# Seeds that stay in PSUM over several gathers, and relu sums divided between ScalarE and VectorE, in a two-layer graph kernel

## The chip, the cores and the metric

The kernel runs on one core of one Trainium2 chip. The metric is the device time in microseconds; the figure of a kernel is the median of its runs. Of the kernel before there are three: 1049.07, 1049.10 and 1049.19 us.

## What is computed

Two graph layers, each followed by a residual sum and a layer norm over 64 features, for 128 graphs ("batches") of 128 nodes. Only the first layer matters here:

```
mask = (adj > 0)
diff = x[:, :, None, :] - x[:, None, :, :]
h    = relu((x @ W1a)[:, :, None, :] + diff @ W1b + b1)      # 192 wide
hm   = einsum('bjkh,bjk->bjh', h, mask)
x    = layernorm(x + hm @ W2 + deg[..., None] * b2)
```

With u = x @ (W1a + W1b) + b1 and v = -(x @ W1b), h is relu(u_j + v_k), summed over the neighbours k of node j. The second layer is a small message-passing step with a gated update; the change does not touch what it computes.

## The kernel before

**Tiling.** Nodes lie on the 128 partitions. Batches go in 32 groups of four (G = 4). The 128 possible neighbours of a node are cut into two halves of 64, and in each half the neighbours are ranked. The first eight of a half (W0) have fixed slots; those beyond go to overflow segments of four slots (W1), 128 segments a batch.

**Values and pieces.** `values` (L539) makes u and v, and 2 x 64 further columns that carry v @ W2/2 and u @ W2/2, in a PSUM tile `pu` of 512 columns, and copies it to `uv`. `pieces` (L556) splits v (with its 64 further columns) into three bf16 tiles b0, b1, b2 whose sum is v: two casts on ScalarE (L563, L569) and two subtractions on GpSimd (L566, L572).

**Picks.** `picks` (L529) makes one-hot bf16 matrices by comparing ranks: `pick0` for the eight fixed slots (from `rankT`), `pick1` for the four overflow slots (from `place`), one VectorE instruction of 512 columns per slot and group. `past` and `own` (L480, L481) say which overflow segment belongs to which node; `own32` is a GpSimd cast of `own` (L487), `ownT` its transpose, `us` the u of each segment's owner (`over`, L602).

**The core: seed, gather, reduce.** For each batch there are six stretches of two slots (C = 2): four of fixed slots, two of overflow slots. For each stretch ScalarE copies u four times (two halves, two slots) into a PSUM tile `pv` of two banks (`seeds`, L597); TensorE adds the neighbours' v by 12 matmuls, pick by piece (`gathers`, L628); VectorE sums the absolute values over the four into a part of 192 columns (`reduces`, L644). There are three `pv` tiles in a ring (`ps_g`, bufs=3), so a seed waits until the reduce three stretches before has read its tile. Relu comes from relu(z) = (z + |z|)/2: the sum of |z| is this path's; the sum of z is linear, and enters in `second` by three matmuls per batch of the mask with the further columns of b0 to b2 (`sums_of_z`, L705, L708), and by a GpSimd product of deg with uv's last columns (`others`, L492). Empty slots hold u alone; `base` (L656) makes their number times |u|, which `together` subtracts.

**Joining.** `together` (L663) is four GpSimd instructions per batch (384, then 192, 192 and 192 columns). `sums` (L677) transposes the part by a matmul and adds the overflow part by `ownT`, and `second` (L296) multiplies by W2, adds the residual and starts the layer norm, half of it on GpSimd. The rest of the tail (`turn`, `message1` to `message3`, `gates`, `update`) is layer two.

**The order** is written out by hand. Each part is a generator; TIMETABLE gives a due time for each of its steps, in units of which PER = 768 make a group, and FIRST and SETUP give those of the beginning. All steps of all groups are sorted by due time and issued in that order, each engine then executing its own instructions in it. Steps of up to seven groups are interleaved. SP issues all loads and stores.

Of the kernel before, what the change touches and what calls it, by code (L numbers as in the profile page):

```python
# [8 lines left out]
F32 = mybir.dt.float32  # L9
# [7 lines left out]
F = 64  # L17
# [4 lines left out]
V = H + F  # L22
W0 = 8
W1 = 4
C = 2
BIGR = 2.0 ** 23
# [3 lines left out]
PER = 768  # L30
TIMETABLE = {
    "load": (-1520,), "masks": (-559,), "ranks": (-122, -122), "degrees": (-402, -367), "turned": (-19, -1),
    "counts": (-114,), "offsets": (-22, -22, 80, 228, 245, 348, 349), "owners": (1039, 1066), "places": (368, 431),
    "pieces": (337, 538, 550, 595), "others": (1085, 1194), "values0": (-55, -50, -37), "values1": (204, 204, 268),
    "pick0": (-44, 50, 88, 133, 133, 137, 251, 419), "pick1": (663, 679, 679, 679), "over0": (578, 602),
    "over2": (1053, 1123), "base0": (693,), "together0": (728, 840, 1185, 1275), "sums0": (1392, 1392, 1405),
    "base1": (708,), "together1": (1189, 1219, 1289, 1289), "base2": (443,), "together2": (1345, 1353, 1370, 1370),
    "sums2": (1443, 1449, 1449), "base3": (717,), "together3": (1408, 1417, 1417, 1417),
    "second": (1425, 1453, 1473, 1502, 1502, 1503), "turn": (1504, 1504), "message1": (1512, 1512),
    "message2": (1534, 1538), "message3": (1539, 1696), "gates": (2002, 2032, 2052, 2068, 2068, 2080),  # L40
    "update": (2201, 2201, 2333, 2396, 2584, 2918, 3390, 3734, 4832),
    "seed": (644, 644, 657, 674, 684, 685, 711, 728, 728, 741, 761, 837, 923, 937, 978, 1149, 1149, 1173, 1203, 1221,
        1271, 1326, 1395, 1397),
    "gather": (661, 661, 681, 681, 686, 708, 730, 730, 737, 748, 767, 940, 1026, 1051, 1110, 1161, 1163, 1189, 1238,
        1317, 1338, 1405, 1405, 1405),
    "reduce": (664, 678, 684, 684, 706, 724, 740, 743, 780, 862, 894, 947, 1119, 1138, 1138, 1192, 1215, 1233, 1263,
        1358, 1358, 1407, 1407, 1407),
# [3 lines left out]
SETUP = (-8001, -7999, -7610, -7530, -7400, -7380, -700, -690)  # L51
FIRST = {
    "load": (-8000, -7998), "masks": (-7580,), "ranks": (-7520, -7515), "degrees": (-7389, -7388), "counts": (-7387,),
    "offsets": (-7372, -7371, -7366, -7366, -7366, -7366, -7365), "turned": (-7359, -7358),
    "values0": (-7375, -7374, -7370), "values1": (-7368, -7364, -7360), "pieces": (-7373, -7363, -7355, -7350),
    "places": (-7357, -7356), "pick0": (-7512, -7512, -7512, -7512, -7365, -7365, -7365, -7365),
    "pick1": (-7352, -7352, -7351, -7351), "over0": (-7349, -7348), "seed": (-7369, -7366, -7361, -7354),
    "gather": (-7367, -7362, -7354, -7351), "reduce": (-7365, -7358, -7353, -7350),
}

# [3 lines left out]
def adj_resnorm_kernel(  # L80
# [42 lines left out]
    wall = const.tile([N, 4 * N], F32, name="wall")  # L123
# [3 lines left out]
    wT = const.tile([HC, 4, 2, F], F32, name="wT")  # L127


    NBI = V + 256 + F  # L130
# [3 lines left out]
    call3, bias3, gb2 = three[:, 0:V], three[:, V : V + 256], three[:, V + 256 : NBI]  # L134
# [27 lines left out]
    def setup(ps_g, ps_w):  # L162
# [8 lines left out]
        for h in range(2):  # L171
            spread(bias[h * F : h * F + 3, 0:H], b1)
            spread(bias[h * F : h * F + 3, H:V], b2)
# [28 lines left out]
        nc.vector.tensor_scalar_mul(wall[:, V : V + H], wab[:, 1, :], -1.0)  # L202
        nc.vector.tensor_copy(iota, ips)
        nc.vector.tensor_scalar_mul(w2c, w2c, 0.5)
        yield

        tps = ps_w.tile([HC, 4, F], F32, tag="w", name="tps")
        for c in range(4):
            cs = (V, V + HC, 0, HC)[c]
            nc.tensor.transpose(tps[:, c, :], wall[0:F, cs : cs + HC], ident[0:F, 0:F])  # L210
        nc.vector.tensor_copy(wT, tps.rearrange("p c (o f) -> p c o f", o=1).to_broadcast([HC, 4, 2, F]))
        yield
        dps = ps_w.tile([N, 2, F], F32, tag="w", name="dps")
        for d in range(2):
            for c in range(2):
                nc.tensor.matmul(dps[:, d, :], wT[:, 2 * d + c], w2c[:, c, :], start=c == 0, stop=c == 1)
        cps = ps_w.tile([N, F], F32, tag="w", name="cps")
        for c in range(2):
            nc.tensor.matmul(cps, b1c[:, c : c + 1].to_broadcast([HC, N]), w2c[:, c, :], start=c == 0, stop=c == 1)
        nc.vector.tensor_copy(wall[:, H:V], dps[:, 0, :])  # L220
        nc.vector.tensor_copy(wall[:, V + H : 4 * N], dps[:, 1, :])
        nc.vector.tensor_add(bias[:, H:V], bias[:, H:V], cps)
        yield
        piece = const.tile([N, NBI], BF16, name="piece")
        three_rows(slice(0, V), piece, at)
        yield

        for t, src in ((gw1, g_w1), (gw2, g_w2)):
            for h in range(2):
                nc.sync.dma_start(t[h * F : (h + 1) * F, h * F : (h + 1) * F], src)  # L230
        spread(bi, b_ih)
# [637 lines left out]
```

## Time and profile before

| what | value |
|---|---|
| median of three runs | 1049.1 us |
| span of the profiled execution | 1047.0 us |
| VectorE (DVE) busy | 972.5 us, 93% |
| TensorE (PE) busy | 952.5 us, 91% |
| ScalarE (ACT) busy | 943.0 us, 90% |
| GpSimd (POOL) busy | 876.6 us, 84% |
| granted TensorE clock, mean | 0.983 |
| HBM traffic | 21.7 MB, 21 GB/s over the span |

The profiled execution's span lies 2.1 us below the runs' median. A row of groups reads: line, engine, operation, out<-in, partitions x elements and type, count | busy us, mean ns of one | idle time of the engine just before them, and whose end stopped most of it. Busy time of a group counts overlapping instructions once. PE's ends are modelled, since matmuls are pipelined, so a busy PE is not one at its peak. The kernel has a long even middle; a window of it shows what one group costs.

### The profile page before, as it was taken

The page shows a single profiled execution, that of the slowest core. Times are in us where ns is not written, and L with a number is a line of the kernel's source. Part 1 is how long each engine was busy: PE and PEld are TensorE (multiplying, and loading weights), DVE is VectorE, ACT ScalarE, POOL GpSimd, SP SyncE. Part 2 cuts the span into 40 slices and gives each one's busy share as a digit, 9 for nine tenths or more (in the row PEclk, how much of TensorE's full clock was granted, in tenths as well). Part 3 has the DMA queues.
Part 4 walks back from the last instruction along what each step waited for, and adds up shares of the span by engine and source line. Part 5 has one row for each costly group of instructions (what it writes and reads, how often), then busy time and mean ns, then how long its engine had stood idle before and what let it go on. Part 6 is the DMA issues. An engine that isn't in the chain of part 4 may idle for free.

```text
span 1047.0 us, 33471 instructions
## 1 busy us (share of the span) xinstructions
PE 952.5 (91%) x13447; PEld 761.0 (73%) x13447; DVE 972.5 (93%) x2202; ACT 943.0 (90%) x1608; POOL 876.6 (84%) x1281
## 2 busy tenths in 40 slices
PE   6798999999999999999999999999999999999984
PEld 3577777777787777777777777777777777777762
DVE  6988999999999999999999999999999999999983
ACT  4789999999999999999999999999999999999971
POOL 2568788889888888988888988988898888898864
PEclk7899999999999999999999999999999999999997
DMA  4000000000000000000000000000000000000000
GB/s 111 1 23 2 23 21 23 28 27 10 19 27 27 27 27 27 3 27 28 26 28 28 4 24 28 27 28 28 24 5 28 27 27 27 27 3 7 7 8 28
DMA packets 21368, 23.95 MB, mean 23 GB/s; under 512 B 4050, under 2 KB 17112, under 8 KB 21208
## 3 DMA queue, kind: packets, MB, share of 16 engines
q1 hardware_dynamic: 21208, 21.76, 7.0%
q8 instruction: 107, 1.75, 0.7%
q14 instruction: 53, 0.43, 0.1%
HBM read 17.55 MB, written 4.19 MB: 21 GB/s over the span
## 4 chain that ended last, share of the span: by engine, by line
PE 31%; DVE 21%; ACT 20%; POOL 20%; issue 7%; DMA 0%; SPq 0%; DVEq 0%; POOLq 0%; ACTq 0%
PE pv L628 12%; ACT pv L597 10%; DVE part L644 10%; PE ph L686 3%; ACT uv L551 3%; POOL part L666 3%; PE pu L544 2%; POOL rs L281 2%; DVE stats L274 2%; DVE pick L534 2%; ACT b L563 2%; PE ph L685 2%; POOL part L670 2%; POOL part L673 2%; POOL r L566 2%
## 5 line engine op out<-in xcount | busy, mean ns | idle before, releaser
L644 DVE TENSOR_REDUCE part<-pv 128x192 f32<-128x768 f32 x768 | 699.6, 949 | 31.6 <-PE pv L628 15.6
L628 PE MATMUL pv<-b,pick 64*128 64x192 bf16 x9216 | 501.6, 244 | 39.1 <-ACT pv L597 34.9
L628 PEld LDWEIGHTS <-pick 64*128 64x128 bf16 x9216 | 385.0, 94 | 123.9 <-issue 94.4
L597 ACT COPY pv<-uv 128x768 f32<-128x768 f32 x512 | 407.5, 804 | 16.6 <-DVE part L644 14.2
L597 ACT COPY pv<-us 128x768 f32<-128x768 f32 x256 | 204.7, 817 | 13.2 <-DVE part L644 13.1
L666 POOL TENSOR_TENSOR part<-part 128x384 f32<-128x384 f32 x128 | 127.8, 998 | 19.7 <-DVE part L644 17.7
L551 ACT COPY uv<-pu 128x512 f32<-128x512 f32 x128 | 75.1, 587 | 27.3 <-PE pu L547 23.1
L544 PE MATMUL pu<-wall,xT 64*128 64x512 f32 x256 | 92.3, 637 | 1.4 <-ACT off L473 1.2
L534 DVE TENSOR_SCALAR pick<-rankT 128x512 bf16<-128x512 bf16 x256 | 88.6, 367 | 1.3 <-ACT rankT L438 1.3
L686 PE MATMUL ph<-ownT,part 128*96 128x128 f32 x512 | 87.6, 273 | 0.2 <-POOL part L673 0.2
L487 POOL CAST own<-own 128x512 f32<-128x512 bf16 x32 | 19.5, 610 | 75.2 <-DVE own L481 69.1
L668 POOL TENSOR_TENSOR part<-part 128x192 f32<-128x192 f32 x128 | 77.3, 604 | 5.1
L572 POOL TENSOR_TENSOR b<-r,b 128x1024 bf16<-128x1024 f32 (+1 forms) x35 | 68.8, 1966 | 12.1 <-ACT b L569 8.9
L670 POOL TENSOR_TENSOR part<-part 128x192 f32<-128x192 f32 x128 | 75.6, 590 | 2.6
L608 PE MATMUL pz<-uv,own 128*128 128x192 f32 x256 | 58.6, 352 | 20.4 <-DVE n L369 12.0
L300 PE MATMUL pw<-w2c,hmT 96*128 96x64 f32 x512 | 75.1, 278 | 0.7 <-ACT hmT L692 0.7
L673 POOL TENSOR_TENSOR part<-part 128x192 f32<-128x192 f32 x128 | 75.5, 590 | 0.0
L300 PEld LDWEIGHTS pw<-w2c,hmT 96*128 96x128 f32 x512 | 69.8, 192 | 6.8 <-issue 4.9
L686 PEld LDWEIGHTS ph<-ownT,part 128*96 128x96 f32 x512 | 70.9, 166 | 1.8 <-POOL part L673 0.7
L685 PE MATMUL ph<-ident,part 128*96 128x128 f32 x256 | 71.0, 277 | 0.8 <-POOL part L670 0.6
L281 POOL TENSOR_TENSOR rs<-ve,nhalf 128x4 f32<-128x4 f32 x64 | 66.7, 1042 | 5.3
L566 POOL TENSOR_TENSOR r<-uv,b 128x1024 f32<-128x1024 f32 x31 | 66.0, 2130 | 0.0
(148 smaller groups left out, 1588.4 us busy)
## 6 DMA issues: line engine op xcount, KB each, us to landing
adjT<-in_adjT_dram SPq DMA_DIRECT2D x32, 256.0 KB, 2.8
xT<-in_xT_dram SPq DMA_DIRECT2D x64, 64.0 KB, 2.6
x<-in_x_dram SPq DMA_DIRECT2D x32, 128.0 KB, 2.4
out_dram<-o SPq DMA_DIRECT2D x32, 128.0 KB, 2.0
wab<-in_w_dram SPq DMA_DIRECT2D x2, 96.0 KB, 2.5
bi<-in_b_ih_dram SPq DMA_DIRECT2D x1, 96.0 KB
bias<-in_b_hh_dram SPq DMA_DIRECT2D x1, 96.0 KB
wx<-in_w_hhT_dram SPq DMA_DIRECT2D x2, 48.0 KB, 3.6
```

Of the source, the lines that this page charges most:

```text
L300: nc.tensor.matmul(p[:, i, :], s["hmT"][:, i, c, :], w2c[:, c, :], start=c == 0, stop=False)
L534: nc.vector.tensor_scalar(s[name][:, i], s[src], 2.0 * (first + i) - 1.0, None, ALU.is_equal)
L544: nc.tensor.matmul(ps[h], s["xT"][ks, i, :], wall[ks, :], start=True, stop=False)
L551: nc.scalar.copy(uv[:, 2 * h + i, :], ps[h])
L597: nc.scalar.copy(v, src.rearrange("p (c b h) -> p c b h", c=1, b=1).to_broadcast(list(v.shape)))
L628: nc.tensor.matmul(v[:, h, j, :], pick[ks, a + j, i, :], s[f"b{c}"][ks, i, F : F + H], start=False, stop=c == 2, skip_group_check=True,)
L644: nc.vector.tensor_reduce(into, view(s["pv", i, k]).rearrange("p c b h -> p h c b"), AX.XY, ALU.add, apply_absolute_value=True,)
L666: nc.gpsimd.tensor_tensor(f[:, 0:2], f[:, 0:2], f[:, 2:4], ALU.add)
L670: nc.gpsimd.tensor_tensor(f[:, 0], f[:, 0], f[:, no], ALU.subtract)
L673: nc.gpsimd.tensor_tensor(f[:, 0], f[:, 0], f[:, 1], ALU.add)
L685: nc.tensor.transpose(p[:, i, c, :], s["part", i0 + i][:, 0, cs], ident)
L686: nc.tensor.matmul(p[:, i, c, :], s["part1", i0 + i][:, 0, cs], s["ownT"][:, i0 + i, :], start=False, stop=True, skip_group_check=True,)
```

## The change

- A `pv` tile is seeded once and used for several gathers. Fixed slots: one seed for two stretches (CH = 2), so two tiles a batch instead of four. Overflow slots: a tile holds two batches, one slot of each in both halves, and one seed serves four gathers, so two tiles a group instead of eight. Seeds a group: 10 instead of 24; gathers: 24 of 12 matmuls, as before.
- So that a later gather replaces the neighbour in the tile, its pick is the difference of two neighbouring picks: `picks` subtracts in place, for `pick0` twice 1024 columns (slots 6-7 less 4-5, 2-3 less 0-1) and for `pick1` three times 512.
- relu is summed as it is. Of each chain (a batch's fixed slots; two batches' overflow slots) ScalarE writes the first stretch's relu, 768 columns, to an SBUF sum `acc` (`keeps`, six a group); VectorE adds the relu of the others with one instruction each (`adds`, 18 a group).
- Therefore the linear path goes: the further columns of `uv` and of the pieces (512 to 384, 1024 to 768 columns), the mask matmuls in `second`, and the setup that made their weights. `base` makes relu(u) times the count; `others` multiplies deg with b2.
- `together` is three GpSimd instructions a batch (384, 192, 192 columns), with a fourth, `joined` (384), for two batches' overflow.
- `past` and `own` are issued as four and then two and two. TIMETABLE, FIRST and SETUP are new throughout, with PER = 100000 units a group; group 0's fixed-slot seeds follow the general table instead of FIRST.

```diff
+CH = 2
-PER = 768
+PER = 100000
...
-    "seed": (644, 644, 657, 674, 684, 685, 711, 728, 728, 741, 761, 837, 923, 937, 978, 1149, 1149, 1173, 1203, 1221,
-        1271, 1326, 1395, 1397),
...
+    "seed0": (39143, 45492, 50871, 62426, 85943, 88416, 104836, 111203),
+    "gather0": (40257, 44606, 47889, 65964, 65964, 70803, 73414, 79243, 88070, 100364, 101018, 107986, 107986,
+        116962, 124137, 127484), "keep0": (41049, 69218, 92410, 111783),
+    "reduce": (45659, 51241, 69750, 71545, 77909, 83855, 102066, 102066, 112143, 125736, 127276, 134462),
+    "seed1": (70395, 113053), "gather1": (74386, 77848, 85675, 95006, 118735, 126920, 135589, 142483),
+    "keep1": (75119, 124808), "reduce1": (80986, 94661, 98205, 132309, 139359, 142770),
...
+                    c = (C, 1)[t]
+                    for a in range(n - c, 0, -c):
+                        if t == 0 and (a // C) % CH == 0:
+                            continue
+                        nc.vector.tensor_tensor(
+                            s[name][:, a : a + c], s[name][:, a : a + c], s[name][:, a - c : a], ALU.subtract
+                        )
+                        yield
...
+        nu = (W0 // C, W1)
+        order = [(i, k) for i in range(G) for k in range(nu[0])], [(q, k) for q in range(G // 2) for k in range(nu[1])]
...
+                for i, k in order[t]:
+                    if k % (CH, W1)[t]:
+                        continue
+                    p = s["pv", t, i, k // CH if t == 0 else 0] = ps_g.tile([N, 2, 512], F32, tag="g", name="pv")
...
-                    nc.vector.tensor_reduce(
-                        into,
-                        view(s["pv", i, k]).rearrange("p c b h -> p h c b"), AX.XY, ALU.add, apply_absolute_value=True,
-                    )
...
+        def keeps(s, t):
+            def part():
+                for i in range((G, G // 2)[t]):
+                    acc = s["acc", t, i] = main.tile([N, 2, C, H], F32, tag=f"acc{t}", name=f"acc{t}_{s['g']}")
+                    nc.scalar.activation(acc, view(s["pv", t, i, 0]), AF.Relu)
                     yield
...
+        def adds(s, t):
+            def part():
+                for i, k in order[t]:
+                    if k:
+                        acc = s["acc", t, i]
+                        nc.vector.scalar_tensor_tensor(
+                            out=acc, in0=view(s["pv", t, i, k // CH if t == 0 else 0]), scalar=0.0, in1=acc, op0=ALU.max, op1=ALU.add
+                        )
+                        yield
...
-                nc.gpsimd.tensor_tensor(f[:, 0:2], f[:, 0:2], f[:, 2:4], ALU.add)
-                yield
                 nc.gpsimd.tensor_tensor(f[:, 0], f[:, 0], f[:, 1], ALU.add)
                 yield
-                nc.gpsimd.tensor_tensor(f[:, 0], f[:, 0], f[:, no], ALU.subtract)
-                yield
-                f = s["part1", i]
+                nc.gpsimd.tensor_tensor(f[:, 0, 0], f[:, 0, 0], f[:, 0, 1], ALU.add)
+                yield
+                nc.gpsimd.tensor_tensor(f[:, 0, 0], f[:, 0, 0], s["nb", i], ALU.subtract)
+                yield
```

## The prediction

> **What bounds the kernel now.** I read the shares of the span first, then the costliest groups, then one steady stretch of the middle, from 400 to 727.2 us, group by group and engine by engine. The page's head and its groups:
>
> ```profile
> PE 952.5 (91%) x13447; PEld 761.0 (73%) x13447; DVE 972.5 (93%) x2202; ACT 943.0 (90%) x1608; POOL 876.6 (84%) x1281
> ...
> L644 DVE TENSOR_REDUCE part<-pv 128x192 f32<-128x768 f32 x768 | 699.6, 949 | 31.6 <-PE pv L628 15.6
> L628 PE MATMUL pv<-b,pick 64*128 64x192 bf16 x9216 | 501.6, 244 | 39.1 <-ACT pv L597 34.9
> ...
> L597 ACT COPY pv<-uv 128x768 f32<-128x768 f32 x512 | 407.5, 804 | 16.6 <-DVE part L644 14.2
> L597 ACT COPY pv<-us 128x768 f32<-128x768 f32 x256 | 204.7, 817 | 13.2 <-DVE part L644 13.1
> L666 POOL TENSOR_TENSOR part<-part 128x384 f32<-128x384 f32 x128 | 127.8, 998 | 19.7 <-DVE part L644 17.7
> ```
>
> No engine stands out: four are between 84% and 93%, and the waits are small and go in a circle (PE for ACT's seed, ACT for DVE's reduce, DVE for PE's gather). The steady stretch says it sharper:
>
> ```profile
> 400.00:600.00 200.00, 187.78 (x2708) 151.50 (x2706) 192.43 (x432) 189.08 (x325) 178.64 (x262) 1.00 0.07 22
> ```
>
> The columns after the length are PE, PEld, DVE, ACT, POOL, the granted clock (1.00: nothing is throttled), and DMA, which is idle. The groups of the stretch 400 to 727.2 hold 254 of a group's 24 reduces, so one group of four batches takes 24 x 327.2 / 254 = 30.92 us. Per group DVE is busy 96.2% of that, 29.75 us; ACT 29.2; PE 29.0; POOL 27.6. So 32 groups are 989.4 us, and 1047.0 - 989.4 = 57.6 us are ramp and tail. DVE bounds it, with 1.2 us a group to spare, and three others close behind: a gain has to relieve all of them.
>
> **The change, part by part**, in us per group. The rows that price it, from the same stretch, first DVE's, then ACT's, PE's and POOL's:
>
> ```profile
> L534 DVE TENSOR_SCALAR pick<-rankT 128x512 bf16<-128x512 bf16 x86 | 30.3, 373 | 0.0
> L481 DVE SCALAR_TENSOR_TENSOR own<-iota,off,past 128x128 bf16<-128x128 bf16 x42 | 14.8, 351 | 1.5
> L305 DVE TENSOR_TENSOR y<-pw,t 128x256 f32<-128x256 f32 x11 | 4.6, 417 | 0.0
> ```
> ```profile
> L551 ACT COPY uv<-pu 128x512 f32<-128x512 f32 x43 | 25.2, 587 | 7.3 <-PE pu L547 5.7
> L347 ACT ACTIVATE mT<-pa 128x256 f32<-128x256 f32 x11 | 4.2, 377 | 0.0
> ```
> ```profile
> L708 PE MATMUL pw<-b,maskT 128*128 128x64 bf16 x132 | 11.1, 192 | 0.0
> ```
> ```profile
> L566 POOL TENSOR_TENSOR r<-uv,b 128x1024 f32<-128x1024 f32 x10 | 21.3, 2131 | 0.0
> L487 POOL CAST own<-own 128x512 f32<-128x512 bf16 x10 | 6.1, 610 | 18.3 <-DVE own L481 18.3
> ```
>
> *Seeds (ACT).* 24 copies into PSUM become 10: a tile of ordinary slots is seeded once for two stretches, one of overflow slots once for four. Two seeds in a row take 1.54 us in the timeline, so one is worth 0.75: -14 x 0.75 = -10.5.
>
> *Keeps (ACT, new).* Six relus of 128x768, PSUM to SBUF. No row has that size; relu at 256 takes 377 ns, a PSUM copy at 512 takes 587, which is 0.82 ns an element more, so 0.80 us, or 0.75 with the overlap: +4.5. ACT also gains 4 narrower uv copies (512 to 384, 0.11 each, -0.4) and two piece casts (1024 to 768, -0.45). ACT: 29.2 - 10.5 + 4.5 - 0.85 = 22.4. It leaves the race.
>
> *Adds for reduces (DVE).* 24 reduces, 0.90 each back to back, go (-21.6); 18 three-operand adds come (a relu and a sum in one, one input in PSUM, one in SBUF). The prologue's rows of that instruction take 480 ns at 256 columns and 550 at 320, and own's 351 at 128: about 1.05 ns an element, like y's. So 768 costs what a reduce does, 0.95, or 0.90 in a row: +16.2. From below, nothing shows two elements a cycle for f32 out of PSUM; from above, an add that waits for the write of the add before it on the same sum (past to own shows 0.1 us) costs up to 18 x 0.1. I take 0. Sum -5.4.
>
> *Differences of picks (DVE, new).* Two subtractions of 1024 and three of 512 bf16 elements, both inputs in SBUF. The trace has no such tensor-tensor row. Lower end, two elements a cycle: 0.68 and 0.42, in sum 2.6, less overlaps 2.3. Upper end, one a cycle as in the own row: 1.22 and 0.68, in sum 4.5. I take 2.3, since the pick row (286 ns for 512 when nothing disturbs it) costs, less the 0.15 us that y's rows at 128 and 256 show as fixed, a quarter of y's price an element: dense bf16 is packed here. There is a rule against them: the Trainium skill, SBUF — State Buffer, section "Who interferes with whom", has a Vector instruction with two SBUF inputs and a reading GpSimd instruction block each other fully. With POOL busy 89% in pieces of about 0.7 us, that is an estimate of 0.3 us per subtraction, 1.6 a group. The row: 86 picks, which by the same section contend too, have a median of 286 and a mean of 373 ns, so 0.09 each. By the row I add 0.5, by the rule 1.6. DVE: 29.75 - 5.4 + 2.3 + 0.5 = 27.2 (28.3 by the rule, 29.4 at one element a cycle).
>
> A second rule speaks against the keeps: ScalarE: Activation LUTs, "Rules for kernel authors", puts relu on VectorE. Obeyed, six more adds make DVE 27.2 + 5.4 = 32.6 and the kernel slower than now. The rows decide: on f32 from PSUM ACT's relu of 256 (377 ns) is no dearer than DVE's pass of 256 (417).
>
> *PE.* The 288 gathers stay. The twelve mask matmuls of L708 (11.1 / 10.58 = 1.05) and a quarter of the pu matmuls (30.7 and 8.9 us in the stretch, so 0.9) go: -2.0, so 27.0. Part of this busy time is pipeline tails, hidden if the next matmul is ready.
>
> *POOL.* Before, 127.8 + 77.3 + 75.6 + 75.5 = 356.2 us, 11.1 a group. After, 4 x (1.00 + 0.60 + 0.59) + 2 x 1.00 = 10.8. The two piece subtractions shrink from 1024 to 768 columns; between 1.00 at 384 and 2.13 at 1024 lies 1.68: -0.9. So 27.6 - 1.2 = 26.4, plus about 1.0 that POOL stands between its own dependent instructions today and 0.3 for sums that now follow each other: 27.7. It is now level with DVE. Counted along its new order, it no longer stands before own32 (1.7 a group today), as four of its 0.6 to 1.5 us pieces come between.
>
> *Order, setup, tail.* Setup loses the folded-weight products; but in the new order the first seed waits for all of group 0's preparation and VectorE's bias rows. Today VectorE gets only four reduces done in the first 33 us, and the last of group 0 at 60.5. Estimated first add at 27 and group 0 done at 56: a draw. I keep 57, with 50 to 65 as bounds. SP issues the same loads and stores less two small bias rows; loads lead by 1.8 group lengths, before by 2.0, for 2.8 us to land. The base's relu for its absolute value, and b2 for a slice of uv in POOL's product, keep kind and size: nothing.
>
> *New waits.* 14 of the 24 gathers now overwrite a sum that a keep or add has still to read. PE waits for it; other tiles' gathers and the small matmuls queued behind wait too, and DVE's adds for those. A round is a gather (0.67 to its end) and two hand-offs of some 0.05 to 0.1 us: 0.8, plus the add itself. In the order nearly all such pairs have another tile's add of 0.9 between them on DVE, and 0.7 to 1.9 us of other matmuls on PE; the thin places are the last two overflow gathers. I allow 0.8 a group for all waits, DVE having 1.2 today.
>
> Sum: the fullest engine 27.7 + 0.8 = 28.5 a group; 57 + 32 x 28.5 = 969 in the profiled execution. The runs' median stands 2.1 above the span today: 971.
>
> **The rivals.**
> *Subtractions at one element a cycle*, or blocked as the rule has it: DVE 29.4 + 0.8 = 30.2, 57 + 966 + 2 = 1025. For it: own's row. Against: the packed picks.
> *The round trips take the reduces' place:* if each of 14 read-before-overwrite waits leaves 0.25 us open on PE, PE is 27.0 + 3.5 = 30.5 and the time 1035. For it: PE already waits 34.9 us for seeds. Against: ACT gets 6.8 us a group of slack, and the distances above.
> *Slower, the ring of three PSUM tiles:* a tile is now held for two or four rounds. By the due times, tiles live 2.14 group lengths in sum, of 3 that the ring has: 61 tile-us of 85. The ring decides from the point where the 24 rounds take 1.3 us longer each than planned (61 + 32 = 93 = 3 x 31); at 1.5 us longer the group is (61 + 36) / 3 = 32.4 and the time 1096. For it: ScalarE executes in order, and a keep behind a late seed stalls all tiles. Against: 29% of the ring is empty, and a round has to be longer than a whole gather and add.
> *Better than thought:* waits vanish, 27.6 a group: 942.
>
> **How the numbers follow.** Likeliest (0.62): 27.8 to 29.4 a group, 949 to 1000, at 971. Below that 0.06. Subtractions dear 0.11, round trips 0.11, ring 0.10. The range 943 to 1028 takes in the likeliest, most of what lies below it, the dear subtractions and half of the round trips, some 0.8; dependent adds at their upper end (1.8 a group) lie in it too. Faster by over 0.2% (about what a measurement can tell from no change) 0.86, within it 0.03, slower 0.11.
>
> **What would show it.** Group length from the adds (18 a group) near 28.5; the add near 950 ns; the 1024 subtraction near 680, or 1220 if I am wrong; the keep near 800; ACT busy near 78%, POOL and DVE above 93%; PE waiting for keeps and adds under 1 us a group. If ACT stays near 90% or DVE waits on gathers above 2 us a group, the hand-offs are the step that failed.

## The result, and the profile after

The changed kernel takes 1064.64 us (median of four runs, 1062.72 to 1064.79), the kernel before 1049.14 beside it: a ratio of 1.0139, 95% interval 1.0124 to 1.0153. It is slower by 15 us, where 971 was forecast. The profiled execution has a span of 1060.7 us, at a mean granted clock of 0.976.

The head of the page, and the groups that answer to those shown before:

```profile
PE 893.6 (84%) x13046; PEld 737.1 (69%) x13047; DVE 1001.7 (94%) x2165; ACT 739.5 (70%) x1352; POOL 859.5 (81%) x1217
...
L627 DVE SCALAR_TENSOR_TENSOR acc<-pv,acc 128x768 f32<-128x768 f32 x576 | 530.0, 946 | 26.7 <-PE pv L605 16.8
L605 PE MATMUL pv<-b,pick 64*128 64x192 bf16 x9216 | 471.7, 245 | 89.2 <-DVE acc L627 52.3
...
L617 ACT ACTIVATE acc<-pv 128x768 f32<-128x768 f32 x192 | 155.7, 811 | 95.0 <-PE pv L605 92.1
L575 ACT COPY pv<-uv 128x768 f32<-128x768 f32 x256 | 206.9, 808 | 21.1 <-DVE acc L627 20.8
L646 POOL TENSOR_TENSOR acc<-acc 128x384 f32<-128x384 f32 x128 | 129.0, 1008 | 31.7 <-DVE acc L627 31.7
```

ScalarE has left the race, from 90% to 70%, as it should. But VectorE, whose 768 reduces gave way to 576 adds of the same length, is busy for longer than before: 1001.7 us against 972.5. The even stretch, with columns PE, PEld, DVE, ACT, POOL, granted clock and DMA:

```profile
400.00:600.00 200.00, 172.84 (x2533) 144.43 (x2533) 194.75 (x421) 142.78 (x262) 167.84 (x238) 0.98 0.08 22
```

VectorE is full (97%). A row that runs once a group, the degree reduction, gives the length of a group. First the changed kernel's, then that of the kernel before (count, shortest, median and longest ns, first and last start):

```profile
L411 DVE TENSOR_REDUCE deg<-pd x27: 154/156/157, 103.5 to 930.1; 128x4 f32<-128x8 f32 x27
```
```profile
L446 DVE TENSOR_REDUCE deg<-pd x28: 154/156/158, 111.6 to 948.6; 128x4 f32<-128x8 f32 x28
```

From 103.5 to 930.1 us in 26 steps is 31.79 us a group; 837.0 us in 27 steps were 31.0 before. So VectorE is busy 31.0 us of each group, where 27.2 was predicted. The chain of waits puts 70% of the span on VectorE:

```profile
DVE 70%; PE 21%; issue 4%; ACT 4%; POOL 1%; SPq 0%; DVEq 0%; DMA 0%; ACTq 0%; POOLq 0%
DVE acc L627 34%; DVE pick L502 14%; PE pv L605 13%; DVE pick L508 6%; DVE past L445 6%; DVE stats L240 3%; ACT pv L575 2%; DVE own L448 2%; PE pz L586 2%; DVE mv L242 2%; PE ph L672 1%; PE pu L520 1%; PE ph L671 1%; DVE y L270 1%; DVE n L334 1%
```

Second after the adds stand the picks, which the change did not touch. Here are VectorE's small SBUF instructions in the stretch 400 to 727.2 of the changed kernel, each form with count, busy us and mean ns:

```profile
L502 DVE TENSOR_SCALAR pick<-rankT 128x512 bf16<-128x512 bf16 x83 | 42.6, 542 | 0.0
L502 DVE TENSOR_SCALAR pick<-place 128x512 bf16<-128x512 bf16 x43 | 24.1, 599 | 0.0
L445 DVE TENSOR_SCALAR past<-iota,off 128x128 bf16<-128x128 bf16 x44 | 23.6, 598 | 0.0
L448 DVE SCALAR_TENSOR_TENSOR own<-iota,off,past 128x128 bf16<-128x128 bf16 x40 | 20.2, 546 | 0.0
L508 DVE TENSOR_TENSOR pick<-pick 128x512 bf16<-128x512 bf16 x32 | 13.2, 414 | 0.0
L508 DVE TENSOR_TENSOR pick<-pick 128x1024 bf16<-128x1024 bf16 x20 | 12.8, 675 | 0.0
```

The two rows at the end are the new subtractions, at two elements a cycle as assumed (0.42 and 0.68). The four above them are unchanged instructions of unchanged size, which took 373, 285, 245 and 351 ns before; the prediction shows the first and the last of these rows, and the two others were:

```profile
L534 DVE TENSOR_SCALAR pick<-place 128x512 bf16<-128x512 bf16 x44 | 10.7, 285 | 0.0
L480 DVE TENSOR_SCALAR past<-iota,off 128x128 bf16<-128x128 bf16 x42 | 10.3, 245 | 0.0
```

What happens to them shows in the timeline (start, length). First VectorE's pick, then what GpSimd did at that time:

```profile
515.93 1.21 DVE L502 TENSOR_SCALAR pick<-rankT 128x512 bf16<-128x512 bf16 x1
```
```profile
515.35 1.65 POOL L542 TENSOR_TENSOR r<-uv,b 128x768 f32<-128x768 f32 x1
```

The pick of 0.28 us begins 0.58 us into GpSimd's subtraction and ends 0.14 us after it: it has stood until the other was through, and the profile counts the standing as busy time. Of the 83 `rankT` picks of the stretch, the 50 that begin while one of GpSimd's wide instructions (192 columns or more) is under way take 0.71 us on average, the 33 others 0.28.

The distance between the two ends is the same again and again. In this stretch 122 picks, `past` and `own` are over 60 ns longer than undisturbed. Of these, 112 end at a fixed distance after the end of a GpSimd instruction: 0.15 us for the 71 picks and eight of the `own`, 0.05 us for the 33 `past`. The other ten are `own` that met GpSimd's 1.5 us comparison for the mask, and all of them end 0.75 us before its end. A control stands beside them: the 183 adds, which read one input from PSUM and one from SBUF, take 914 to 959 ns whatever GpSimd does.

I call the lengthening **standing**: mean less undisturbed duration, times the number in a group. Undisturbed are 0.285 for a pick, 0.245 for past, 0.345 for own, 0.414 and 0.675 for the subtractions. After: 8 x 0.257 + 4 x 0.314 + 4 x 0.353 + 4 x 0.201 = 5.5 us a group. Before: 8 x 0.088 and nothing for the others, 0.7.

### The profile page after: what moved, and what is told of

It reads as the page before. It is cut to its first block, busy times and chain, and to the rows that moved or that the text cites. A ratio compares the mean times of both kernels' runs of the same rounds, so it can differ in the third digit from the quotient of the medians.

```text
span 1060.7 us, 32124 instructions
## 1 busy us (share of the span) xinstructions
PE 893.6 (84%) x13046; PEld 737.1 (69%) x13047; DVE 1001.7 (94%) x2165; ACT 739.5 (70%) x1352; POOL 859.5 (81%) x1217
## 4 chain that ended last, share of the span: by engine, by line
DVE 70%; PE 21%; issue 4%; ACT 4%; POOL 1%; SPq 0%; DVEq 0%; DMA 0%; ACTq 0%; POOLq 0%
DVE acc L627 34%; DVE pick L502 14%; PE pv L605 13%; DVE pick L508 6%; DVE past L445 6%; DVE stats L240 3%; ACT pv L575 2%; DVE own L448 2%; PE pz L586 2%; DVE mv L242 2%; PE ph L672 1%; PE pu L520 1%; PE ph L671 1%; DVE y L270 1%; DVE n L334 1%
## 5 line engine op out<-in xcount | busy, mean ns | idle before, releaser
L627 DVE SCALAR_TENSOR_TENSOR acc<-pv,acc 128x768 f32<-128x768 f32 x576 | 530.0, 946 | 26.7 <-PE pv L605 16.8
L605 PE MATMUL pv<-b,pick 64*128 64x192 bf16 x9216 | 471.7, 245 | 89.2 <-DVE acc L627 52.3
L617 ACT ACTIVATE acc<-pv 128x768 f32<-128x768 f32 x192 | 155.7, 811 | 95.0 <-PE pv L605 92.1
L575 ACT COPY pv<-uv 128x768 f32<-128x768 f32 x256 | 206.9, 808 | 21.1 <-DVE acc L627 20.8
L646 POOL TENSOR_TENSOR acc<-acc 128x384 f32<-128x384 f32 x128 | 129.0, 1008 | 31.7 <-DVE acc L627 31.7
L575 ACT COPY pv<-us 128x768 f32<-128x768 f32 x64 | 51.4, 803 | 101.7 <-DVE acc L627 101.7
L520 PE MATMUL pu<-wall,xT 64*128 64x384 f32 x256 | 63.4, 548 | 51.0 <-DVE y L270 49.7
L650 POOL TENSOR_TENSOR acc<-acc,nb 128x192 f32<-128x192 f32 x128 | 76.6, 598 | 23.4 <-ACT nb L638 18.4
L672 PE MATMUL ph<-ownT,acc 128*96 128x128 f32 x512 | 89.2, 273 | 1.9 <-POOL acc L658 1.9
L508 DVE TENSOR_TENSOR pick<-pick 128x512 bf16<-128x512 bf16 (+1 forms) x160 | 82.8, 533 | 0.1
L648 POOL TENSOR_TENSOR acc<-acc 128x192 f32<-128x192 f32 x128 | 77.5, 605 | 2.6
L527 ACT COPY uv<-pu 128x384 f32<-128x384 f32 x128 | 54.8, 480 | 27.5 <-PE pu L523 27.5
L671 PE MATMUL ph<-ident,acc 128*96 128x128 f32 x256 | 72.4, 283 | 1.9 <-ACT b L545 1.2
L658 POOL TENSOR_TENSOR acc<-acc 128x384 f32<-128x384 f32 x64 | 65.6, 1025 | 2.4 <-DVE acc L627 1.4
```

The costliest lines, as they stand in the source:

```text
L508: nc.vector.tensor_tensor(s[name][:, a : a + c], s[name][:, a : a + c], s[name][:, a - c : a], ALU.subtract)
L520: nc.tensor.matmul(ps[h], s["xT"][ks, i, :], wall[ks, :], start=True, stop=False)
L575: nc.scalar.copy(v, src.to_broadcast(list(v.shape)))
L605: nc.tensor.matmul(v[:, h, j, :], pick[ks], s[f"b{c}"][ks, gr, :], start=False, stop=c == 2, skip_group_check=True,)
L617: nc.scalar.activation(acc, view(s["pv", t, i, 0]), AF.Relu)
L627: nc.vector.scalar_tensor_tensor(out=acc, in0=view(s["pv", t, i, k // CH if t == 0 else 0]), scalar=0.0, in1=acc, op0=ALU.max, op1=ALU.add)
```

## The experiments

Two theories go through the expectations. The port theory (theory 1): VectorE and GpSimd block each other at a port that they share, instruction by instruction, and that standing is what makes VectorE full. The round-trip theory (theory 2): gathers wait for the add or keep that reads their tile, adds for gathers, and a late one sets the group. This table holds what all twelve gave; runs 1, 2 and 3 were timed once, the others at least four times. The group is measured on the same row as above, standing worked out as above, DVE busy is its share of 400 to 727.2 times the group.

| kernel | time, us | group, us | standing, us | DVE busy, us |
|---|---|---|---|---|
| before | 1049.1 | 31.0 | 0.7 | 29.8 |
| changed kernel | 1064.6 | 31.8 | 5.5 | 31.0 |
| no joins on GpSimd | 999.5 | 29.8 | 2.7 | 28.2 |
| more GpSimd work | 1060.1 | 31.6 | 4.6 | 30.1 |
| no differences | 1024.5 | 30.5 | 5.5 | 28.6 |
| before, own32 late | 1134.3 | 33.8 | 4.1 | 33.0 |
| own together | 1131.7 | 34.0 | 3.1 | 28.7 |
| own after the pow | 1074.4 | 32.1 | 4.7 | 30.1 |
| past off the port | 1056.5 | 31.5 | 4.9 | 30.8 |
| joins on PE and ACT | 1104.1 | 33.0 | 5.2 | 30.7 |
| three blocks | 1290.6 | 39.3 | 2.2 | 28.7 |
| pick1 later | 1052.3 | 31.5 | 5.0 | 30.6 |
| past on ScalarE | 1049.2 | 31.2 | 5.7 | 30.5 |
| both of these | 1041.0 | 31.0 | 5.0 | 30.0 |

No time fell into the range that the port theory gave for it, and two (runs 2 and 9) into that of the round-trip theory. So the times alone decide for neither theory. What the runs show lies in the rows: which instruction stood, and for how long.

**1. GpSimd with less to do.** Two of `together`'s adds and `joined` are left out, the sums of the output with them.

```diff
-                nc.gpsimd.tensor_tensor(f[:, 0], f[:, 0], f[:, 1], ALU.add)
-                yield
-                nc.gpsimd.tensor_tensor(f[:, 0, 0], f[:, 0, 0], f[:, 0, 1], ALU.add)
+                yield
...
                 f = s["acc", 1, q]
-                nc.gpsimd.tensor_tensor(f[:, 0], f[:, 0], f[:, 1], ALU.add)
```

> Leaves out the two additions of together and the one of joined, so that only a quarter of each sum reaches the output; takes 4 x 1.6 + 2 x 1.0 = 8.4 us a group off GpSimd and nothing off the other engines. Theory 1 (VectorE instructions that take the port shared with GpSimd stand until the GpSimd instruction under way has ended): the means of pick (542 and 599 ns), past (598) and own (546) fall at least halfway to their undisturbed 286, 285, 244 and 351, VectorE loses 2.5 to 3.5 us a group, the span falls from 1061 to 950-985. Theory 2 (round trips between gather and add set the length; GpSimd is in none of them): the span stays within 1055-1066, and the rows stay long.

Measured: one run, 999.5 us. The same VectorE rows:

```profile
L502 DVE TENSOR_SCALAR pick<-rankT 128x512 bf16<-128x512 bf16 x88 | 34.4, 420 | 0.0
L445 DVE TENSOR_SCALAR past<-iota,off 128x128 bf16<-128x128 bf16 x44 | 17.6, 460 | 0.0
```

No VectorE instruction was taken away, and yet VectorE's busy time fell by 2.8 us a group, as much as the standing fell (5.5 to 2.7). So GpSimd's instructions cost VectorE time. The gain of 65 us is smaller than the port theory's range (950 to 985 us): with 8.0 of GpSimd's 27 us a group gone, half of the standing is left.

**2. GpSimd with more to do.** Two further adds of 384 columns a group, into a tile that nobody reads.

```diff
                 nc.gpsimd.tensor_tensor(f[:, 0], f[:, 0], f[:, 1], ALU.add)
+                e = main.tile([N, C, H], F32, tag="extra", name=f"extra{s['g']}")
+                nc.gpsimd.tensor_tensor(e, f[:, 0], f[:, 1], ALU.add)
```

> Adds two GpSimd additions of 384 columns a group (2.0 us) whose result nobody reads; GpSimd stands idle for 16% of a group, 5 us, so as a load they fit in. Theory 1 (shared port): pick, past and own collide more, VectorE's busy time grows by 0.6 to 1.5 us a group, span 1080-1110. Theory 2 (round trips): nothing waits for them, 1058-1064.

Measured: one run, 1060.1; GpSimd's busy share of the stretch rose from 84% to 95%, and the time did not. The port theory's expectation (1080 to 1110) failed, and the time is the round-trip theory's: with more load, standing did not grow here, it fell from 5.5 to 4.6. And it moved:

```profile
L508 DVE TENSOR_TENSOR pick<-pick 128x1024 bf16<-128x1024 bf16 x20 | 19.3, 1002 | 0.0
...
L445 DVE TENSOR_SCALAR past<-iota,off 128x128 bf16<-128x128 bf16 x44 | 8.1, 248 | 0.0
```

past is undisturbed here, and the wide subtractions stand 0.33 us each instead. Which instruction meets which had changed.

**3. No subtractions.** The five differences are left out, so that later gathers add the wrong neighbours.

```diff
-                    for a in range(n - c, 0, -c):
+                    for a in range(0):
```

> Leaves out the five subtractions of picks, so that later gathers of a tile add whole picks; all waits of the round trips stay. Theory 1 (VectorE full, its length made by the port): VectorE loses their 2.6 us a group and the span falls to 970-990; the other pick rows stay above 450 ns. Theory 2 (round trips): the same handshakes stay, span 1045-1062.

Measured: one run, 1024.5, between the two ranges. The subtractions are worth 1.3 us a group, half of their 2.6 of busy time; the old instructions keep standing (own 573 ns, and these):

```profile
L502 DVE TENSOR_SCALAR pick<-rankT 128x512 bf16<-128x512 bf16 x84 | 41.3, 531 | 0.0
L445 DVE TENSOR_SCALAR past<-iota,off 128x128 bf16<-128x128 bf16 x43 | 22.9, 593 | 0.0
```

So the standing doesn't come from the instructions that the change adds.

**4. The kernel before, with one step moved.** GpSimd's cast `own32` comes 151 of 768 units later in the timetable. Nothing else is edited.

```diff
-    ... "offsets": (-22, -22, 80, 228, 245, 348, 349), ...
+    ... "offsets": (-22, -22, 80, 228, 245, 348, 500), ...
```

> The kernel before, with one step moved: GpSimd's cast of own is due at 500 instead of 349, so GpSimd doesn't stand (1.7 us a group) while VectorE makes past and own. Theory 1 (shared port): that standing was the cover; past (244) or own (351) get longer by 0.1 to 0.3 us each and meet GpSimd's work, 1060-1100 us, though no wait and no work was added. Theory 2 (a wait of a nearly full engine is a cost): 1035-1050.

Measured: 1134.3, ratio 1.0809 (1.0791 to 1.0827), 85 us slower: the way the port theory had it, and beyond its 1100. VectorE's rows in the stretch:

```profile
L534 DVE TENSOR_SCALAR pick<-rankT 128x512 bf16<-128x512 bf16 x80 | 48.0, 620 | 0.0
L481 DVE SCALAR_TENSOR_TENSOR own<-iota,off,past 128x128 bf16<-128x128 bf16 x40 | 20.6, 515 | 1.4
L480 DVE TENSOR_SCALAR past<-iota,off 128x128 bf16<-128x128 bf16 x40 | 17.1, 428 | 0.0
```

The old algorithm now has long rows as the new kernel has them, the picks from `place` excepted (284 ns). GpSimd's idle time before own32 was 18.3 us in the stretch, 1.7 a group, spent waiting while VectorE made most of `past` and `own` undisturbed. With the step moved, 3.4 us of standing come, VectorE's busy time rises by 3.2 and the group by 2.8. About 1.8 of the 3.4 stand on `past`, `own` and the one pick that had run during the wait: to these the wait had been cover, though it looked like loss on GpSimd. The other 1.6 are one later pick, which now meets GpSimd's piece subtraction of 2.1 us (it takes 1.90 us, for instance from 421.50) and had met nothing before: GpSimd's later instructions had shifted.

**5 and 6. The wait put back in the changed kernel.** Order only. First `own` and `own32` directly after `past`:

```diff
-    ... "offsets": (-50790, -49646, -45752, -29607, -19699, -6073),
+    ... "offsets": (-50790, -49646, -45752, -45752, -45752, -45752),
```

> Only the order: the four own and GpSimd's cast of them follow directly on the four past, so that GpSimd comes to stand at its cast while VectorE makes past and own, as in the kernel before. Theory 1 (shared port): past falls from 598 to about 250 ns and own from 546 to about 350, 2.2 us a group less on VectorE, GpSimd again waits 1.5 to 2.5 us a group for own; some of it comes back in picks that now meet GpSimd's work: 990-1035. Theory 2 (round trips): 1055-1066.

Then `past`, `own` and `own32` all behind the first norm's statistics, where GpSimd has work of 4 columns:

```diff
-    ... "offsets": (-50790, -49646, -45752, -29607, -19699, -6073),
+    ... "offsets": (-50790, -49646, -30200, -30180, -30160, -28200),
```

> Only the order, of the changed kernel: past and own follow VectorE's first layer-norm statistics and one add, and GpSimd's cast of own follows the power that it computes from them (1.04 us on 4 columns), before its long instructions. Unlike the first reordering, t4, which VectorE's y waits for, stays ahead of the cast. Theory 1 (shared port): past falls to 250-300 ns and own to 350-400, 2 us a group off VectorE, GpSimd waits 1-2 us for own: 1000-1040. If VectorE or TensorE come to wait for x1, some is lost: up to 1055. Theory 2: 1055-1066.

Measured: 1131.7 (ratio 1.078, 1.0762 to 1.0798) and 1074.4 (1.023, 1.0207 to 1.0254). In both, past and own are back at 246 and 344 ns, and in both the time is worse, above the ranges of both theories. The waits of the first of the two, over the whole execution, with total us, number and longest, say where it went:

```profile
POOL own L455 <- DVE own L448: 125.8, 31, 5.5
PE pu L520 <- DVE y L270: 122.8, 30, 4.3
...
DVE y L270 <- POOL t L462: 89.9, 30, 3.2
```

In the changed kernel the first two are 2.7 and 49.7 us. GpSimd waits for own with everything behind it, among that the sum `t` that VectorE's `y` needs, and `y` holds up the next values on PE: a new wait took the standing's place. (The clock granted to PE is 0.95 in the stretch of this run, against 0.98, which may add to it.) In the second, the `rankT` picks met GpSimd instead (669 ns). Freeing past and own was not enough in either, against the port theory's expectation of a gain.

**7. past in a form that stays off the port.** The accumulating form of the same comparison, with a sum that is not used.

```diff
-                    nc.vector.tensor_scalar(s["past"][:, i, :], iota, off[:, 1, i : i + 1], None, ALU.is_ge)
+                    nc.vector.tensor_scalar(
+                        s["past"][:, i, :], iota, off[:, 1, i : i + 1], 0.0, ALU.is_ge, ALU.add, accum_out=junk[:, i : i + 1]
+                    )
```

> The four past comparisons also write a sum that nobody reads, which by the Trainium skill (SBUF, Who interferes with whom) takes this form off the port shared with GpSimd, at one element a cycle instead of four: 0.10 us dearer each if undisturbed. Theory 1 (waits for the shared port): past falls from a mean of 598 ns, 245 to 767, to a nearly constant 340-360, VectorE gains about 0.6-0.9 us a group, 1030-1050 us. Theory 2 (something else stretches VectorE's bf16 rows, or the round trips set the length): past gets longer by 100 ns, 1063-1070.

Measured: 1056.5, ratio to before 1.0063 (1.0046 to 1.008), between the two ranges and 8 us below the changed kernel. past's own line (duration min, median, max), first in the changed kernel and then here:

```profile
L445 DVE TENSOR_SCALAR past<-iota,off x44: 245/688/767, 403.2 to 723.2; 128x128 bf16<-128x128 bf16 x44
```
```profile
L446 DVE TENSOR_SCALAR_CACHE_REDUCE past<-iota,off x44: 335/343/344, 403.1 to 719.1; 128x128 bf16<-128x128 bf16 x44
```

This is the cleanest evidence for the port. In the same place of the order, against the same GpSimd instructions, the comparison took 245 to 767 ns with a median of 688; this slower form takes 343 and is never disturbed, though all 44 run beside GpSimd's wide instructions. Of the 1.4 us of standing saved, 0.8 is passed on: the `rankT` picks rise from 542 to 610 ns, the small subtractions from 414 to 477. Each of the four costs 0.10 us more in this form and brings a second instruction of 0.08 that reads the sum out, so that VectorE's busy time falls by 0.2 us a group only. (The same section of the Trainium skill that the prediction used says that the accumulating form keeps off the shared pair; these 343 ns agree.)

**8. GpSimd's work moved to engines with slack.** `together`'s second add and the subtraction of the base become accumulating matmuls, and own32's cast goes to ScalarE.

```diff
-                nc.gpsimd.tensor_copy(s["own32"], s["own"])
+                nc.scalar.copy(s["own32"], s["own"])
...
-                nc.gpsimd.tensor_tensor(f[:, 0, 0], f[:, 0, 0], f[:, 0, 1], ALU.add)
-                yield
-                nc.gpsimd.tensor_tensor(f[:, 0, 0], f[:, 0, 0], s["nb", i], ALU.subtract)
...
                         nc.tensor.transpose(p[:, i, c, :], s["acc", 0, i0 + i][:, 0, 0, cs], ident)
+                        nc.tensor.matmul(
+                            p[:, i, c, :], s["acc", 0, i0 + i][:, 0, 1, cs], ident, start=False, stop=False,
...
+                            p[:, i, c, :], s["nb", i0 + i][:, cs], nident, start=False, stop=False,
...
```

> Takes short instructions off GpSimd and keeps the result: the second addition of together and the subtraction of the base become accumulating matmuls beside the transposes (16 a group, about 1.8 us of TensorE), and own is cast on ScalarE: 5.4 us a group off GpSimd. Theory 1 (shared port): fewer collisions, VectorE loses 1.5-2.5 us a group, 985-1030. Theory 2 (round trips through TensorE set the length): TensorE gets fuller, 1062-1100.

Measured: 1104.1, ratio 1.0524 (1.0506 to 1.0541): slower than the changed kernel, where the port theory had it faster, and just above the round-trip theory's 1100. Stretch and `past`:

```profile
400.00:727.20 327.20, 303.35 (x4357) 259.41 (x4352) 304.23 (x657) 233.30 (x427) 218.89 (x289) 1.00 0.08 22
```
```profile
L447 DVE TENSOR_SCALAR past<-iota,off 128x128 bf16<-128x128 bf16 x40 | 21.4, 597 | 0.0
```

GpSimd is busy 67% of the time, and past stands as before (597 ns); in run 2 it was 95% and past stood at nothing. Load and standing do not go together here: the meetings come from the order of the instructions, which repeats every group. Run 1 left GpSimd busy 63%, partly by taking away other instructions, and halved the standing. PE, at 93% and 30.6 us a group instead of 27.5, pays for the new matmuls.

**9. All meetings avoided at once.** VectorE's `past`, `own`, picks and differences are put into three blocks, opposite GpSimd's 4-column instructions and waits, with one gather, one add and the transposes of x1 moved along; nothing is added or left out.

```diff
-    ... "offsets": (-50790, -49646, -45752, -29607, -19699, -6073),
+    ... "offsets": (-50790, -49646, -33800, -33700, -33690, -28200),
...
-    "pick0": (-44549, -42307, -40365, -28334, -4416, -3828, -3828, 7614, 16799, 22780),
...
+    "pick0": (-33940, -33930, -33920, -33910, 27300, 27310, 27320, 27330, 27340, 27350),
...
```

> The changed kernel with another order of the same instructions, made for theory 1 (shared port): VectorE's comparisons and subtractions that take the port are gathered in three blocks, each opposite a stretch in which GpSimd has only instructions on 4 columns or stands at a wait: the overflow picks opposite the second norm's power, past, own, four picks and three subtractions opposite the first norm's power and before GpSimd's cast of own, the other picks and both wide subtractions opposite the counts. TensorE's transposes of x1 come later, so that they don't wait for it. Theory 1: pick 290-400 ns, past 250-350, own 350-400, 3 to 4.5 us a group less on VectorE, of which 1 to 2 come back as waits of VectorE and TensorE behind the longer blocks: 985-1035. Theory 2 (round trips between gather and add set the length, the port is only a symptom): the blocks make the round trips worse, above 1065.

Measured: 1290.6, ratio 1.2304 (1.2281 to 1.2327).

```profile
L445 DVE TENSOR_SCALAR past<-iota,off 128x128 bf16<-128x128 bf16 x32 | 5.9, 249 | 0.0
```
```profile
PE pv L605 <- DVE acc L627: 217.1, 143, 4.4
DVE acc L627 <- PE pv L605: 207.1, 166, 2.9
```

Standing falls to 2.2 and VectorE's busy time to 28.7, as the port theory has it; and PE and VectorE now wait for each other over 200 us each (52.3 and 16.8 in the changed kernel), as the round-trip theory has it. While VectorE works off a block, no tile is read, and no gather may overwrite one. (The clock granted to PE falls to 0.86 in the stretch, which may add to that.) Both theories have a part: in these orders, standing is what the fine interleaving costs that the round trips need.

**10 to 12. Two small edits, and both.** The four comparisons of places go behind two adds:

```diff
-    "pick1": (44490, 45646, 45646, 48148, 54565, 55816, 70861), ...
+    "pick1": (51300, 51310, 51320, 51330, 54565, 55816, 70861), ...
```

> The changed kernel in which only the four comparisons of places (pick1) move: they stand in a row behind two adds, opposite GpSimd's 4-column instructions of the normalisation, instead of between them. No instruction is added or left out. Port theory: the picks from place take about 290 to 350 ns instead of 599, so VectorE gains about 1.1 us a group of its 5.5, if nothing else moves into their place: 1030 to 1050. Round-trip theory: four comparisons in a row are 1.2 us in which no add runs, twice what a gather's round has to spare, so PE and VectorE wait for each other and the time is 1065 to 1100.

`past` moves to ScalarE, which is busy 71%:

```diff
+                neg = prep.tile([N, G], F32, tag="neg", name=f"neg{g}")
+                nc.scalar.activation(neg, p[:, 1, :], AF.Copy, bias=100.0, scale=-200.0)
...
-                    nc.vector.tensor_scalar(s["past"][:, i, :], iota, off[:, 1, i : i + 1], None, ALU.is_ge)
+                    nc.scalar.activation(s["past"][:, i, :], iota, AF.Sigmoid, scale=200.0, bias=neg[:, i : i + 1])
```

> The changed kernel with past computed on ScalarE, as a steep sigmoid of iota less the offset (exactly 0 or 1 in bf16), instead of VectorE's comparison; one more ScalarE copy makes the bias. Four VectorE instructions of 598 ns go (2.4 us a group), five of about 0.25 us come on ScalarE, which is busy 71%. Port theory: half of the 2.4 us comes back as standing of other instructions, as with the comparison taken off the port (8 us of 11): a group of 30.4 to 31.0, 1015 to 1035. Round-trip theory: VectorE's time is not what sets the group; the order of keeps on ScalarE slips by 1.2 us and the time stays at 1050 to 1075.

> Both of these edits together: past on ScalarE, and the four comparisons of places moved behind two adds. Port theory: 3.5 us a group less on VectorE, about half of it kept: 1000 to 1030, below the kernel before. Round-trip theory: as the moved comparisons alone, 1060 to 1100.

Measured: 1052.3 (ratio to before 1.0031, 1.002 to 1.0041), 1049.2 (0.9999, 0.999 to 1.0007), and 1041.0 with both (0.9923, 0.9906 to 0.9939). The first lies between its two ranges, just above the port theory's 1050. The second fell between the two ranges, just below the round-trip theory's: more of what it freed came back as standing than the half I had allowed (2.4 us of past gone, 0.6 of group gained). The last lies between its two ranges as well; it is faster than both kernels, than the one before by 0.8%. Its rows show the passing on:

```profile
L504 DVE TENSOR_SCALAR pick<-rankT 128x512 bf16<-128x512 bf16 x87 | 61.1, 732 | 0.0
...
L504 DVE TENSOR_SCALAR pick<-place 128x512 bf16<-128x512 bf16 x40 | 8.9, 284 | 0.0
```

The place picks are undisturbed, and the `rankT` picks stand 0.45 us each. Its group is that of the kernel before (31.0); the gain over it lies in ramp and tail, the beginning and end outside the even middle (1039.2 - 32 x 30.98 = 48 us against 1047.0 - 992 = 55).

## Why the prediction was wrong

**Most of the sums were right, the fullest engine was not.** The prediction's sum ends with GpSimd as the fullest engine, at 27.7 us, and VectorE at 27.2. In the run VectorE is at 31.0 and GpSimd, at 84%, waits. ScalarE: predicted 22.4 us a group, measured 142.78 / 200 x 31.79 = 22.7; a keep 0.80, measured 0.81. PE 27.0 against 27.5. An add 0.95 against 0.946, so adds that follow each other on one sum cost nothing extra, as taken. There was luck in it: by the 1.05 ns an element that the prediction read off the rows of that instruction, 768 columns would cost 1.02 (0.351 + 640 x 1.05 ns), and the 0.95 was the reduce's. The subtractions 0.68 and 0.42 against 0.675 and 0.414, so the rival with one element a cycle is out. GpSimd's busy time 26.4 against 26.7, a piece subtraction 1.68 against 1.65. Ramp and tail: 1060.7 - 32 x 31.79 = 43 us, 14 better than the 57 taken and better than my bounds of 50 to 65. So the whole miss is the group: 31.8 against 28.5, 3.3 us x 32 = 106 us, less those 14.

**The step that failed** is "By the row I add 0.5, by the rule 1.6", together with "it no longer stands before own32 (1.7 a group today)". The rule (the Trainium skill, SBUF — State Buffer, section "Who interferes with whom": one shared pair of ports, held for a whole instruction, the other engine blocked fully) was weighed for the five new subtractions alone. They do not stand in the changed kernel. It is the 20 old instructions, whose price I carried over from the trace of before, that stand 5.5 us a group, against 0.7. Predicted 27.2, less the 0.5 for the port, is 26.7; with 4.8 more standing it is 31.5, and 31.0 was measured. This case's traces agree with the rule in 112 of the 122 long rows, which end with GpSimd's instruction; in the ten that came through in the middle of the mask's comparison the hold did not last for the whole instruction.

Why the row misled: the 0.09 us a pick was a true mean, but of one order. In that order most of past and own ran while GpSimd stood before own32, and the place picks (285 ns) met nothing that blocks. I saw that wait, counted its end as a gain for GpSimd, and did not ask whom it had protected. That it would end was right: before own32 GpSimd waits 2.7 us in the whole execution, where it had waited 69.1. Run 4 shows what such a step is worth: moving it in the old kernel brings 3.4 us of standing, half of it on what the wait had covered, and 85 us. The same section's full blocking, taken over all 25 instructions at the 0.3 us I had worked out for one, is an estimate of 7.5 us a group for an order with no cover. In place of the 0.7 that the old rows hold, VectorE's sum would have been 26.7 - 0.7 + 7.5 = 33.5: above the 31.0 measured, and on the right side.

**The rivals.** The rival "Subtractions at one element a cycle", or "blocked as the rule has it", had in its second half the right mechanism on the wrong instructions. Its 1025 is the price of the first half; for the blocking alone the prediction's own 28.3 gives 57 + 32 x (28.3 + 0.8) + 2 = 990. The round trips were not the bound, nor was the ring of three tiles. The waits in 400 to 727.2 us, 10.3 groups:

```profile
ACT pv L575 <- DVE acc L627: 40.4, 28, 3.0
...
PE pv L605 <- DVE acc L627: 15.2, 39, 0.9
PE pv L605 <- ACT pv L575: 9.7, 17, 0.9
...
DVE acc L627 <- PE pv L605: 4.8, 12, 0.4
```

PE waits 1.5 us a group for adds and 0.9 for seeds, more than the 0.8 allowed, but VectorE waits only 0.5 for gathers, and PE is busy 86%. Where the order changes they can become it: run 9 shows that. ScalarE waits 3.9 us a group for adds to free a tile, and at 71% busy it can afford that. The forecast's slower case, 0.10, thus rested on a mechanism that did not come, and the one that came had been given no slower case.

**What stays open.** In the twelve versions of the changed kernel standing is between 2.2 and 5.7 us, and where VectorE was relieved by an edit it stayed near 5. That fits a full VectorE running against GpSimd's fixed sequence, since an instruction that stands less starts the next one earlier, into the next GpSimd piece. That reading is argued, not shown. A kernel with the change's instructions, no standing and intact round trips was not found, so whether 28.5 a group would follow from that has not been tested; the nearest is run 1, with 29.8 at 2.7 us of standing, and it leaves ten of GpSimd's adds a group out. The granted clock in the stretch is 0.98 for the changed kernel and 1.00 for most others; what that alone does to the time was not separated. Where the 14 us of ramp and tail were gained was not traced.

## What to carry to other kernels

The price of a VectorE instruction on SBUF that GpSimd can block belongs to an order, not to the instruction: when a change brings a new order, take its undisturbed duration and add the blocking for all such instructions, the unchanged ones too. A wait of one engine may be cover for another; before counting its end as a gain, look at what the other engine executes during it. Where such standing is found, giving an instruction to another engine (past on ScalarE) or a form that GpSimd does not disturb shortened the group here by about a quarter of what it freed (0.6 of 2.4 us and 0.3 of 1.4), and the rest passed to other instructions or into the form's own cost.

## What the hardware showed unexpectedly

- Blocking goes both ways: while two 1024-column subtractions ran from 518.70 to 519.97 us, GpSimd's 4-column `rnd` took 0.56 us and `nseg` 0.51, against 0.24 and 0.23 in the kernel before. It does so in every group.
- A blocked instruction does part of its work while it stands. Undisturbed, a pick takes 0.28 us, past and own 0.245 and 0.345; blocked, they end 0.15, 0.05 and 0.15 us after GpSimd. An estimate from the prices an element in the prediction (1.05 ns, a quarter of it for pick and past) gives 0.13, 0.03 and 0.13 us for their elements alone, so the fixed part seems to be over by then.
- One GpSimd instruction let VectorE through in its middle: the mask's comparison of 1.5 us. In the changed kernel ten `own` end 0.75 us before its end; in the kernel before, eleven picks do.
- The accumulating form of the comparison (343 ns at 128 columns) is dearer than the plain one (245) undisturbed, and cheaper than it where GpSimd is in the way (598), even with the 84 ns for reading the sum out.
- GpSimd at 95% busy left `past` at 248 ns, GpSimd at 67% had it at 597: with a fixed order, meetings repeat in every group.
